# A transformer block with routed experts: another hand-written order for its beginning and its end, and the first sequence's q and k heads scaled on GpSimd

## The chip, the core and the metric

The kernel runs on one core of a Trainium2 chip. Its time is the device time of one execution in microseconds (us). TensorE (PE in the profile) multiplies matrices, VectorE (DVE) and ScalarE (ACT) read PSUM and SBUF, GpSimd (POOL) works on SBUF here, and SyncE (SP) issues DMA. Every engine takes its own instructions in the order in which the program gives them, and semaphores between engines make one wait for another.

## What is computed

Sixteen sequences of 256 tokens of width 256 pass through one attention block with 16 heads of 64. Then all 4096 tokens pass a routing step in which each of 8 experts picks its 512 best tokens:

```python
shift = jax.nn.silu(t) @ W_ada.T + b_ada
h = _ln(x, ln1_g, ln1_b) + shift
qkv = (h @ Wqkv.T).reshape(b, n, 3, H, HD)
q = _ln(q part, qn_g, qn_b); k = _ln(k part, kn_g, kn_b); v = v part
attn = softmax(q k^T / sqrt(HD)); x = x + (attn v) @ Wout.T
gate = softmax(tok @ Wgate.T, axis=-1)
vals, idx = top_k(gate.T, k_cap)
g = _ln(tok[idx_flat], mlp_g, mlp_b)
y = gelu(g @ fc1 + b1) @ fc2 + b2
tok = tok.at[idx_flat].add(y * w)
```

## The kernel before

All products are float32. The weights of q and k are first centred per head (`center`, L552 and L553, VectorE), so that the head's mean is already gone from the projection and only its variance is missing.

For each sequence, `First` normalises the two tiles of 128 tokens, transposes them (L597) and evicts them as `hT` (L605, ScalarE). A `Group` is one projection of 128 tokens to 512 columns, that is 8 heads: groups 0 and 1 are q, 2 and 3 are k, 4 and 5 are v. A v group is a matmul (L631) and a copy (L640). A q or k group has up to eight steps: `matmul` (L631), `square` (L644, ScalarE), `stats` (L648 and L652, VectorE), `power` (the power of -1/2, L82, GpSimd), `scale` (L664), `transposes` (L673), `evict` to `qT` or `kT` (L685, ScalarE), and, if an eighth place is given, `keep`: a copy of the projection from PSUM to SBUF (L626, ScalarE). `scale` looks whether `keep` has run. If it has not, VectorE multiplies straight out of PSUM, and if it has, GpSimd multiplies the copy:

```python
engine, src = nc.gpsimd, self.qk
if src is None:
    self.qk = work.tile([P, GW], F32, tag="qk", bufs=3, name="qk")
    engine, src = nc.vector, self.pm
```

A `Quad` is four heads in two pairs: scores (L706), row maxima (L713, VectorE), exponentials with their sums (L722, ScalarE), the inverse of the sums (L729), the normalising (L733, GpSimd), the transposes of the probabilities (L742), their copy out of PSUM (L750 on VectorE, L752 on ScalarE), the product with v (L760) and an eviction (L772, L770). A `Tail` projects 128 tokens back (L784), adds the residual (L791), writes the token to `out`, normalises it for the experts (L573) into `xn_dram`, and computes its gate logits (L806, L812, L817, L823).

PSUM has eight banks in this kernel: three buffers with the tag "mm" for projections and small transposes, four with the tag "sc" for scores, transposed probabilities and the experts, one with the tag "po".

The routing runs twice. Before the last sequence, the `first` search finds for each expert the 256th largest gate among the first 15 sequences: 30 steps of compare (L901, VectorE), count (L956, a small matmul), and `either` and `decide` (L962 and L971, VectorE), each waiting for the one before. `masks`, `scans`, `totals`, `place`, `turn_places` and `split` (L981 to L1025) then give each chosen token its place, one-hot columns (L1083 on VectorE, L1080 and L1081 on ScalarE) and small matmuls (L1091) turn the places into a list of token numbers, and a `Job` gathers the rows of `xn_dram` (L1107, GpSimd's queue), multiplies (L1116, L1135, L1142, L1151) and adds the result to `out` (L1168). There are 16 jobs: 8 experts on the first list, 8 on the second. The search and the first list stand beside the attention of the last sequence, and the second routing beside the first jobs, in an order that the code fixes.

The order of everything up to the first job is a plan written out by hand. Each step has a place, a number, and the steps are recorded in the order of their places. `STEADY` gives the places of one sequence, repeated with a period of 55.238. `START` replaces those of the sequences 0 to 3, `END` those of 12 to 15, and further tables (`SHIFT`, `CENTER`, `LOADS`, `EARLY`, `GATES`, `TURN`, `LOAD`, `SEARCH`, `PLACE`, `LIST`, `UP`, `DOWN`) place the rest. `FILL` sets how many transposes of a constant are put in at four points of the beginning.

## Time and profile before

| what | us |
|---|---|
| median of 3 runs (lowest to highest) | 1189.59 (1186.35 to 1192.12) |
| the profiled execution, device time | 1187.28 |
| its span, first to last instruction | 1185.6 |
| TensorE busy | 1157.4 |
| VectorE busy | 759.0 |
| ScalarE busy | 630.4 |
| GpSimd busy | 585.4 |

The profile is of one execution. Busy times are sums over instructions. The ends of matmuls are modelled, so the distance between the starts of two matmuls says more than their length. A waiting engine is put down to what released it last. In a row of busy times by stretch, the clock is what TensorE was granted as a share of full speed, followed by the share of DMA time and GB/s.

The mean granted clock is 0.994. The first matmul starts at 1.44 us, the search's first count stands at 864.89 us and its last at 906.96 us, the first expert's first matmul at 930.49 us.

### The profile page before, as it was taken

Reading aid. Unit: us, or ns where it says so; the run is one execution under the profiler, and the core shown is the slowest. Engines: PE = TensorE matmul, PEld = TensorE weight load, DVE = VectorE, ACT = ScalarE, POOL = GpSimd, SP = SyncE. Lnnn points to the kernel's source line nnn. Section 1 sums busy time; section 2 is a strip of 40 time slices with the busy share of each in tenths; the row PEclk is TensorE's granted clock in tenths of the full one; section 3 lists DMA queues with packets and bytes.
Section 4 is the critical chain, followed back from the end, with each engine's and each line's share of the span. In section 5 each row is a group of like instructions: output and inputs, shape, how many; then the busy total and the mean of one; then the engine's idle time right before and its main releaser. Section 6 shows DMA issues by size and latency. Waiting matters only on the chain. (4 is left out here: it accounts for less than half of the span.)

```text
span 1185.6 us, 19672 instructions
## 1 busy us (share of the span) xinstructions
PE 1157.4 (98%) x6823; PEld 817.5 (69%) x6823; DVE 759.0 (64%) x2303; ACT 630.4 (53%) x1721; POOL 585.4 (49%) x813
## 2 busy tenths in 40 slices
PE   8999999999999999999999999999988899999996
PEld 5566666666666666666666666677745788888885
DVE  7665676667566666666666666565588578755540
ACT  3856655566565656565655565656566333233331
POOL 3665464556556455555555545463672143333332
PEclk9999999999999999999999999999999999999998
DMA  6000000000000000000000000000110365666661
GB/s 197 1 1 6 5 19 19 10 19 10 19 23 6 23 10 19 10 23 6 23 10 27 10 10 9 19 14 19 61 39 1 113 190 183 187 187 187 183 187 21
DMA packets 46740, 62.41 MB, mean 53 GB/s; under 512 B 3889, under 2 KB 39985, under 8 KB 46641
## 3 DMA queue, kind: packets, MB, share of 16 engines
q1 hardware_dynamic: 36864, 49.03, 12.4%
q0 software_dynamic: 6144, 8.39, 3.9%
q10 hardware_dynamic: 3632, 3.74, 1.0%
q8 instruction: 54, 0.88, 0.3%
q14 instruction: 46, 0.37, 0.1%
HBM read 48.56 MB, written 12.58 MB: 52 GB/s over the span
## 5 line engine op out<-in xcount | busy, mean ns | idle before, releaser
L631 PE MATMUL pm<-wq,hT 128*128 128x512 f32 x768 | 361.8, 600 | 2.2 <-ACT qT L685 0.9
L733 POOL TENSOR_SCALAR pr<-pr,sums 128x256 f32<-128x256 f32 x512 | 236.9, 480 | 208.3 <-DVE sums L729 160.9
L82 POOL TENSOR_TENSOR ss<-ss,neghalf 128x8 f32<-128x8 f32 x128 | 211.8, 1656 | 184.7 <-DVE ss L652 180.0
L722 ACT ACTIVATE pr<-sc,nmax 128x256 f32<-128x256 f32 x512 | 236.2, 474 | 115.9 <-DVE nmax L713 108.3
L631 PEld LDWEIGHTS pm<-wq,hT 128*128 128x128 f32 x768 | 133.6, 190 | 123.4 <-issue 109.9
L713 DVE TENSOR_REDUCE nmax<-sc 128x2 f32<-128x512 f32 x256 | 166.7, 684 | 38.2 <-PE sc L706 38.1
L648 DVE TENSOR_REDUCE ss<-sq 128x8 f32<-128x512 f32 x128 | 87.4, 683 | 109.9 <-ACT sq L644 109.4
L742 PEld LDWEIGHTS pp<-ident,pr 128*128 128x128 f32 x1024 | 119.1, 142 | 48.2 <-POOL pr L733 21.0
L742 PE MATMUL pp<-ident,pr 128*128 128x128 f32 x1024 | 139.2, 274 | 0.1
L644 ACT ACTIVATE sq<-pm 128x512 f32<-128x512 f32 x128 | 76.7, 600 | 113.5 <-PE pm L631 110.1
L706 PE MATMUL sc<-kT,qT 64*128 64x256 f32 x1024 | 129.3, 390 | 0.0
L760 PE MATMUL po<-prT,v 128*64 128x256 f32 x1024 | 126.1, 389 | 0.0
L706 PEld LDWEIGHTS sc<-kT,qT 64*128 64x128 f32 x1024 | 93.3, 186 | 41.9 <-issue 31.1
L784 PE MATMUL pw<-wo,oT 128*128 128x256 f32 x512 | 117.8, 383 | 0.0
L1135 PE MATMUL ph<-xT,w 128*128 128x256 f32 x512 | 117.5, 382 | 0.0
L1151 PE MATMUL py<-w,hid 128*128 128x256 f32 x512 | 116.5, 380 | 0.0
L1168 POOL DMA_INDIRECT out<-y,idx x32 | 51.4, 1605 | 124.8 <-DVE y L1162 57.7
L784 PEld LDWEIGHTS pw<-wo,oT 128*128 128x128 f32 x512 | 96.7, 192 | 18.7 <-issue 6.5
L722 ACT ACTIVATION_READ_ACCUMULATOR pr<-sc,nmax 128x1 f32 x512 | 105.0, 205 | 0.0
L1142 ACT ACTIVATE hid<-ph,vec 128x256 f32<-128x256 f32 x128 | 60.2, 473 | 83.3 <-PE ph L1135 75.8
L1135 PEld LDWEIGHTS ph<-xT,w 128*128 128x128 f32 x512 | 95.4, 190 | 12.9
L1151 PEld LDWEIGHTS py<-w,hid 128*128 128x128 f32 x512 | 95.5, 190 | 12.7
(136 smaller groups left out, 1294.1 us busy)
## 6 DMA issues: line engine op xcount, KB each, us to landing
w<-in_fc2T SPq DMA_DIRECT2D x16, 1024.0 KB
w<-in_fc1T SPq DMA_DIRECT2D x16, 1024.0 KB
out<-tok SPq DMA_DIRECT2D x32, 128.0 KB
xn_dram<-tn SPq DMA_DIRECT2D x32, 128.0 KB
xs<-in_x SPq DMA_DIRECT2D x12, 256.0 KB
b<-in_b2s SPq DMA_DIRECT2D x16, 128.0 KB
wq<-in_wqkvT SPq DMA_DIRECT2D x3, 512.0 KB
wq<-in_wqkvT ACTq DMA_DIRECT2D x3, 512.0 KB
```

What stands on the lines that cost most here:

```text
L82: nc.gpsimd.tensor_tensor(dst, src, neghalf[:, : src.shape[1]], ALU.pow)
L631: nc.tensor.matmul(self.pm, hTs[self.b][:, c, bass.ts(self.t, P)], wq[:, c, bass.ts(self.g, GW)], start=(c == 0), stop=(c == DC - 1),)
L648: nc.vector.tensor_reduce(self.ss[:, 0, :], self.sq.rearrange("p (h d) -> p h d", d=HD), AX.X, ALU.add,)
L706: nc.tensor.matmul(self.sc[i, j][:, t, :], qTs[self.b][rows, hp, bass.ts(t, P)], kTs[self.b][rows, hp, :], start=True, stop=True,)
L713: nc.vector.tensor_reduce(self.nmax[i, j], self.sc[i, j], AX.X, ALU.max, negate=True)
L722: nc.scalar.activation(self.pr[i, j][:, t, :], self.sc[i, j][:, t, :], AF.Exp, bias=self.nmax[i, j][:, t : t + 1], scale=1.0, accum_out=se ...
L733: nc.gpsimd.tensor_scalar(self.pr[i, j][:, t, :], self.pr[i, j][:, t, :], self.sums[i][:, 1, j, t : t + 1], 1.0, ALU.mult, ALU.mult,)
L742: nc.tensor.transpose(self.pp[i, j][:, c, bass.ts(t, P)], self.pr[i, j][:, t, bass.ts(c, P)], ident,)
L760: nc.tensor.matmul(self.po[j * HD : (j + 1) * HD, i, :], vs[self.b][:, c, bass.ts(4 * self.d + 2 * i + j, HD)], self.prT[i, j][:, c, :], s ...
L784: nc.tensor.matmul(self.pw, oTs[self.b][:, hp, bass.ts(self.t, P)], wo[:, hp, :], start=(hp == 0), stop=(hp == HP - 1),)
L1135: nc.tensor.matmul(self.ph[f], self.w1[:, c, bass.ts(f, P)], self.xT[:, c, :], start=(c == 0), stop=(c == DC - 1),)
L1151: nc.tensor.matmul(self.py[i], self.hid[:, f, bass.ts(i, P)], self.w2[:, f, :], start=(f == 0), stop=(f == FC - 1),)
```

## The change

Numbers in the tables change, and no statement of the code. The tables `START` and `END` and all the further tables named above but `FILL` get new values (`STEADY` keeps its own), so the same steps stand in another order on each engine. Sequence 0's q and k groups get an eighth place, which means that `keep` is called: its eight projections are copied out of PSUM by ScalarE and scaled by GpSimd, where VectorE scaled them in PSUM. Sequence 15 does this already. The number of matmuls, transposes and fills is the same.

```diff
     START = {
         0: dict(
-            first=((-139.487, -139.084, -130.002), (-134.729, -123.135, -95.026), (-71.635, -61.204)),
+            first=((-133.593, -101.058, -97.256), (-158.376, -131.500, -104.051), (-81.952, -81.887)),
             group={
-                (0, 0): (-59.500, -57.180, -53.990, -41.905, -41.892, -31.199, -19.864),
-                (0, 1): (-56.514, -46.937, -42.187, -36.541, -32.975, -14.723, -12.430),
+                (0, 0): (-80.466, -69.038, -57.316, -39.709, -38.352, -36.469, -35.382, -52.242),
+                (0, 1): (-60.059, -54.606, -54.600, -39.627, -32.905, -30.429, -30.229, -51.780),
...
-    CENTER = ((-64.072, -68.386), (-36.649, -27.859), (-57.938, -59.128), (-18.701, -14.089))
+    CENTER = ((-91.311, -88.593), (-42.094, -51.590), (-84.871, -62.797), (-31.921, -44.332))
     FILL = (16, 4, 8, 12)
-    LOADS = (-61.203, -19.863)
+    LOADS = (-81.886, -35.381)
...
         15: dict(
...
             group={
-                (0, 0): (825.134, 835.486, 837.594, 846.062, 859.856, 877.526, 889.953, 847.485),
+                (0, 0): (839.140, 843.782, 846.873, 846.892, 851.911, 861.206, 869.747, 844.619),
...
-    EARLY = {14: (894.209, 902.691,), 15: (1025.834, 1032.355,)}
+    EARLY = {14: (910.717, 915.638,), 15: (1023.715, 1024.870,)}
...
-    PLACE = (1019.174, 1020.931, 1020.932, 1022.153, 1023.809, 1025.004, 1047.220)
+    PLACE = (1021.098, 1022.519, 1022.468, 1022.566, 1022.818, 1022.832, 1028.390,)
     LIST = (
-        dict(gives=1025.018, onehot=(1025.083, 1025.087, 1026.657, 1025.278, 1026.694, 1025.819,),
-             matmul=(1026.115, 1026.244, 1026.688, 1026.735, 1027.886, 1029.466,),
-             then=(1031.034, 1032.801, 1036.028, 1040.565,)),
+        dict(gives=1023.577, onehot=(1023.251, 1022.838, 1023.479, 1023.758, 1022.884, 1024.282,),
+             matmul=(1023.940, 1023.984, 1024.390, 1024.426, 1024.476, 1024.739,),
+             then=(1024.875, 1024.926, 1025.818, 1025.854,)),
```

On TensorE the beginning keeps its order up to the first q projection. Then five projections stand ahead of the first q/k transposes, where four stood. In the search, steps that had one transposed probability tile beside them now have two or none. Behind the search, the first job's list and its row transposes stand closer together, with less of the last projection between them: 0.86 us of it by the spacing of such matmuls in the profile, and the rest ahead of the second list.

## The prediction

> **What bounds the kernel now.** I read the page's busy shares first, then the same shares by stretch, then TensorE's waits, then its instructions in order of time.

> ```profile
> span 1185.6 us, 19672 instructions
> ...
> PE 1157.4 (98%) x6823; PEld 817.5 (69%) x6823; DVE 759.0 (64%) x2303; ACT 630.4 (53%) x1721; POOL 585.4 (49%) x813
> ```

> TensorE is busy for 98% of the span, and the change neither adds nor removes a matmul, a fill or a transpose. So only TensorE's lost time can move. A busy share hides part of that, because ends are modelled; I therefore price TensorE by the distance between starts. In time order, six 128x512 matmuls (two passes each) start at 31.86 us and the next group at 37.10: about 0.86 us per matmul when nothing waits. Likewise 0.109 us per 128x128 transpose, 0.22 per scores or value matmul, 0.43 per 128x256 expert or projection matmul. Counts times these give 1112 us; 73 us of the span are lost. In the steady middle the loss is about 1 us in 20, and the order of sequences 4 to 11 does not change. What stands out is the beginning and the stretch of the first threshold search.

> ```profile
> 10.00:20.00 10.00, 8.46 (x26) 3.69 (x24) 9.40 (x20) 2.41 (x5) 4.49 (x3) 1.00 0.41 151
> 20.00:30.00 10.00, 8.35 (x38) 4.72 (x40) 8.23 (x18) 5.28 (x9) 3.48 (x3) 1.00 0.61 185
> 30.00:40.00 10.00, 9.62 (x45) 5.11 (x42) 9.15 (x19) 8.00 (x26) 6.82 (x8) 1.00 0.01 2
> ```

> Columns: length, then busy PE, weight load, DVE, ACT, POOL, then clock. VectorE is nearly full, ScalarE and GpSimd are not: VectorE ends the waits here.

> ```profile
> PE pc L956 <- DVE reach L901: 7.1, 16, 0.8
> PE pls L1091 <- ACT oh L1081: 3.3, 5, 1.5
> ...
> PE pq L673 <- DVE qk L664: 1.3, 2, 1.0
> ...
> PE pm L631 <- ACT qT L685: 0.9, 1, 0.9
> ...
> PE pm L631 <- DVE wq L553: 0.7, 1, 0.7
> PE pm L631 <- DVE qk L664: 0.7, 1, 0.7
> ```

> The last four lines are the beginning, three of them VectorE's centring and scaling. The first two are the search and the job list behind it.

> ```profile
> 898.50:902.00 3.50, 2.74 (x24) 1.69 (x21) 3.32 (x16) 2.42 (x11) 1.58 (x5) 1.00 0.00 0
> 902.00:905.40 3.40, 2.12 (x16) 1.46 (x15) 2.89 (x16) 2.47 (x7) 1.36 (x3) 1.00 0.00 0
> 905.40:908.90 3.50, 2.35 (x18) 1.49 (x18) 3.20 (x17) 2.25 (x4) 1.84 (x4) 1.00 0.02 5
> 908.90:912.30 3.40, 3.40 (x18) 1.73 (x15) 1.58 (x5) 0.33 (x1) 0.00 (x0) 0.50 0.00 0
> ...
> 919.00:922.50 3.50, 0.72 (x4) 0.38 (x4) 0.45 (x2) 3.29 (x11) 0.00 (x0) 1.00 0.00 0
> 922.50:925.90 3.40, 3.40 (x23) 2.86 (x24) 2.77 (x18) 0.00 (x0) 2.00 (x2) 0.51 0.11 27
> ```

> The clock is granted at half twice (0.50 and 0.51), each time for 3.4 us after thinly filled stretches, costing some 1.7 us each on top of the waits.

> **The beginning.** For sequence 0, eight scalings (8 x 0.68 = 5.4 us) leave VectorE. In exchange ScalarE copies the projection out of PSUM and GpSimd scales the copy. Both steps exist in sequence 15 of this trace:

> ```profile
> L626 ACT COPY qk<-pm x8: 580/584/620, 833.6 to 872.5; 128x512 f32<-128x512 f32 x8
> L664 POOL TENSOR_TENSOR qk<-qk,ss x8: 1042/1042/1228, 835.3 to 877.4; 128x512 f32<-128x512 f32 x8
> ```

> So ScalarE gets 8 x 0.58 = 4.7 us and GpSimd 8 x 1.05 = 8.4 us. What matters is the PSUM buffer: "mm" has three. Before, a projection held one until square, statistics, power (1.65 us on GpSimd) and scaling were over: TensorE idles until 17.83 for `qk`, and until 20.79 for the first q/k transposes. After, it is held only until square and copy. I walked the new orders by hand with these durations and 0.2 to 0.3 us per hop. The first q projection starts at 10.9 instead of 11.75, as its first half of wq is now centred first. Five projections then run without a gap to 19.5. The first transposes start at 19.9: GpSimd does two powers (15.4 to 18.7) before the first scaling (to 19.8). The second half of the q weights is centred late, at 22.9: 0.95 us lost. The transposes of sequence 1 start at 35.4 with 30.2 us of work ahead of them, 5.1 lost; in the trace 41.29 with 32.4 ahead, 8.9 lost.

> Then part is given back. In the work from 20 to 40 us of TensorE, ScalarE's queue holds 23.8 us against 19.0 before. Behind its copies stand the evictions of q and k, of sequence 1's `hT`, and the exponentials that free the four "sc" buffers. I find 1.1 us lost at `hT` and 1.1 at the scores of quad 1. The four DMA issues in ScalarE's queue (0.4 to 0.5 us each) are moved too, past the v copy and a square; that is in the walk. At 41.5 us of work the loss is 7.4; before, 9.2: 1.8 gained, with bounds of 4 (nothing given back) and -2 (each hop longer by 0.2).

> [...] The row above has its worst scaling 0.19 us over its best, beside a VectorE busy with other operations; no centring ran beside it. [...]

> **Sequences 1 to 3 and 12 to 14.** The work of each engine per 20 us of TensorE work stays within the bounds of the steady middle, except GpSimd at 780 to 800 (19.4 against 11.8; less after it: 7.5 against 16.8). The old order lost only about 1 us in 20 here, so there is nothing to win; I take zero, up to 3 us lost. The loads of `xs` on SP move with them; the last is issued at 741.5 and first read at 769.8, 28 us of cover.

> **The search.** One step (L956, decide, compare) with 0.44 us of TensorE work beside it takes 1.12 to 1.16 us: VectorE's chain 0.28 + 0.54 + 0.09 and the hops. With 0.88 beside it 1.17, with 1.72 1.83, with 1.76 about 2.0. The old order takes 42.07 us between the first and last counting matmul, with 26.2 us of work beside them. The new one has 26.1 us, spread otherwise: only 7 steps of 29 with 0.44 (15 before), more with 0.87, and three with none at all where a maximum (0.68) sits in the chain. My sum is 41.4: 0.7 gained, bounds 3 and -2. Places alone save little, as the chain is VectorE's.

> **From the last count to the second expert.** Before, the first expert's list completes 16.0 us after the last count, because ScalarE's ten one-hot columns (0.63 each) wait at 915.52 for a PSUM eviction that TensorE orders late. After, five of them stand ahead of that eviction and start as soon as the places are split. The place matmul now waits for the scans with nothing beside it (2.1 to 3.6 after the last count: 1.5 lost). Split to 5.6, five columns to 8.8, eviction 0.6, five more to 12.5: list complete at 12.6, with TensorE nearly idle from 9.3. Then the projection (3.4), list two (waits 0.5 for VectorE's last column), 0.9 of projection: 18.4. Meanwhile take (0.3), two gathers (issued at 13.2 and 14.8, 3.4 to landing) make the rows at 18.2, so no wait; the eviction costs 0.3 more. The same point (the second expert's down matmuls, 954.78, or 47.8 after the last count) comes at 41.8, with 0.9 less work in it: 5.1 gained. The second expert's weights are issued on SP after the last projection, at 18.5; 2.1 MB at the 290 to 370 GB/s of the stretch 930 to 938 are 7 us and some 2 to start, so 28, and they are needed at 33.9.

> The clock decides how much remains. [...] I take 3.4.

> Sum: 1.8 + 0.7 + 3.4 = 5.9 us. The profiled execution took 1187.28 us (its span 1185.6 and 1.7 around it), 2.3 under the median of the runs, 1189.59. So 1181.4 for such an execution, and 1183.7 for the median.

> **The rivals.** (1) All of it holds: no half clock behind the list (1.7 more) and nothing given back to ScalarE at the start (2 more): 1180.0. For it: waits are short. Against it: the clock rows, and 23.8 us of ScalarE in 20. (2) The end's gain is spent: a second halving (1.7), and gathers landing 1.7 late because little stands between list and first rows: 1183.7 + 3.4 = 1187.1. Before, six us of projection covered them. (3) Slower: ScalarE's in-order queue at the start. In the first 50 us it was idle for 22.9, waiting mostly for projections. If copies placed ahead of evictions wait in turn, idle does not shrink while work to 40 us grows from 33.5 to 37.6: that point comes at 22.9 + 37.6 = 60.5 instead of 51.0, 9.5 us late; less the end's 4.1, 1195.0. It decides once ScalarE gives up less than 5.4 of its idle 22.9. Against it: seven of its waits (11.3 us, for projections) shrink when TensorE no longer waits for VectorE.

> **How the numbers follow.** The sum above 0.50 (1179 to 1188 by the bounds); rival 1 0.22; rival 2 0.15; rival 3 0.13. A measurement of this kernel can tell some 0.5% from no change: faster by over that is under 1183.6. That holds for rival 1 and half of the first case: 0.47; slower 0.13 (rival 3); within it 0.40. The range, 1177 to 1190, leaves out rival 3 and some of the far end.

> **What would show it.** The first q projection near 10.9 us and no TensorE wait for `qk` before 19; sequence 1's first transposes near 35; ScalarE over 90% busy from 30 to 45. First to last count 41 to 42 us. The list's end 12 to 13 us after the last count, one stretch of half clock after it. I am wrong if TensorE waits in sequences 12 to 14, or if the scalings on GpSimd take clearly over 1.05 us.

## The result and the profile after

| | before | after |
|---|---|---|
| median of five runs each (lowest to highest), us | 1190.09 (1186.35 to 1192.12) | 1183.99 (1182.07 to 1186.23) |
| profiled execution, us | 1187.28 | 1182.07 |

The ratio is 0.9952, with a 95% interval of 0.9936 to 0.9969: 0.3 to 0.6% faster. The forecast was 1183.7 us.

Executions of one kernel differ by how long the clock is halved in them: of the 51 runs of before that stand beside the experiments below, the 21 of at most 1188.12 us had a mean granted clock of 0.994 or 0.995 and the other 30 (1188.19 to 1192.12 us) one of 0.990 to 0.993, so ratios are safer than single times.

The page's span and busy shares:

```profile
span 1180.3 us, 19683 instructions
...
PE 1155.7 (98%) x6823; PEld 816.9 (69%) x6823; DVE 755.3 (64%) x2295; ACT 632.7 (54%) x1729; POOL 593.2 (50%) x821
```

VectorE has eight instructions less, ScalarE and GpSimd eight more each, TensorE the same number; its busy time falls by 1.7 us, which is what one stretch of half clock less (3.4 us) would give. The gain is lost time of TensorE, counted as in the prediction (distance between starts less the spacing of such a matmul), by stretch:

| TensorE's lost time, us | before | after | difference | predicted |
|---|---|---|---|---|
| start to 60 us | 8.15 | 6.19 | -1.96 | -1.8 |
| 60 us to the first count | 38.20 | 38.42 | +0.22 | 0 |
| first count to last count | 15.24 | 13.59 | -1.65 | -0.7 |
| last count to the second expert's down matmuls | 10.62 | 8.96 | -1.66 | -3.4 |
| the rest | 3.17 | 3.16 | 0 | 0 |
| sum | 75.38 | 70.32 | -5.06 | -5.9 |

The beginning, busy time by stretch (length, then TensorE, weight load, VectorE, ScalarE, GpSimd, then the clock):

```profile
10.00:20.00 10.00, 10.00 (x35) 4.94 (x34) 9.66 (x20) 4.29 (x8) 4.61 (x4) 1.00 0.41 150
20.00:30.00 10.00, 8.80 (x32) 4.43 (x31) 7.61 (x19) 6.36 (x12) 9.46 (x9) 1.00 0.58 186
30.00:40.00 10.00, 10.00 (x49) 5.67 (x48) 6.60 (x16) 9.08 (x24) 9.04 (x9) 1.00 0.00 1
40.00:50.00 10.00, 10.00 (x53) 6.03 (x52) 6.51 (x14) 9.54 (x35) 7.26 (x13) 1.00 0.00 0
```

Read it against the three rows of before: TensorE has no gap from 10 to 20, where it had 1.54 us. From 20 on GpSimd is full and from 30 on ScalarE is, the two engines that took VectorE's scalings; TensorE is full beside them, so they are close to the bound but not over it.

TensorE's waits (us in total, times, longest):

```profile
PE pc L956 <- DVE reach L901: 6.7, 10, 1.0
PE pls L1091 <- ACT oh L1081: 1.7, 4, 0.5
PE px L1116 <- DMA xg<-xn_dram,idx: 1.6, 1, 1.6
...
PE pm L631 <- ACT v L640: 1.2, 1, 1.2
PE pplace L1013 <- DVE place L1004: 1.0, 1, 1.0
```

All waits for VectorE's scaling and centring are gone; the list's wait for ScalarE's columns is halved. New are the projection's wait at 23.2 us behind the copy of v and that of the place matmul behind the scans. The wait for the second expert's rows has grown from 0.8 to 1.6 us; the prediction's sum has no term for it, and it is most of what is missing at the end. In before it was:

```profile
PE px L1116 <- DMA xg<-xn_dram,idx: 0.8, 1, 0.8
```

The transfers and that wait in after, in order of time:

```profile
923.43 1.00 POOL L1107 DMA_INDIRECT xg<-xn_dram,idx  x1 [2.40 <-DVE w L1102]
...
924.15 0.38 SPq L1053 DMA_DIRECT2D w<-in_fc2T  x1
924.59 0.73 SPq L1055 DMA_DIRECT2D w<-in_fc1T  x1
924.74 0.95 POOL L1107 DMA_INDIRECT xg<-xn_dram,idx  x1 [0.30 <-issue]
...
931.86 0.33 PE L1116 MATMUL px<-ident,xg 128*128 128x128 f32 x1 [1.57 <-DMA xg<-xn_dram,idx]
```

The two gathers and the 2 MB of weights between them are all the second expert's. Its second gather is issued behind the weights and its rows come 7.1 us later. The weights themselves came in time.

One stretch of half clock is left behind the list. The rows are cut at the moments at which the clock changes, and at the same distance before them (the clock is the third figure from the end):

```profile
906.47:909.88 3.41, 2.39 (x22) 1.80 (x23) 2.31 (x6) 1.56 (x3) 0.35 (x1) 1.00 0.00 0
909.88:913.29 3.41, 3.41 (x22) 2.57 (x18) 3.37 (x21) 3.20 (x11) 0.54 (x2) 1.00 0.00 0
913.29:916.70 3.41, 1.74 (x31) 1.07 (x29) 3.11 (x19) 3.25 (x11) 0.00 (x0) 1.00 0.02 5
916.70:920.12 3.42, 3.21 (x9) 2.58 (x10) 2.86 (x15) 0.16 (x1) 2.21 (x2) 0.50 0.13 36
```

### The profile page after: what moved, and what is told of

The parts are those of the page before. It is cut to its first block, busy times and chain, and to the rows that moved or that the text cites. A ratio compares the mean times of both kernels' runs of the same rounds, so it can differ in the third digit from the quotient of the medians.

```text
span 1180.3 us, 19683 instructions
## 1 busy us (share of the span) xinstructions
PE 1155.7 (98%) x6823; PEld 816.9 (69%) x6823; DVE 755.3 (64%) x2295; ACT 632.7 (54%) x1729; POOL 593.2 (50%) x821
## 3 DMA queue, kind: packets, MB, share of 16 engines
q1 hardware_dynamic: 36864, 49.03, 12.5%
## 5 line engine op out<-in xcount | busy, mean ns | idle before, releaser
L631 PE MATMUL pm<-wq,hT 128*128 128x512 f32 x768 | 360.5, 599 | 1.2 <-ACT v L640 1.2
L631 PEld LDWEIGHTS pm<-wq,hT 128*128 128x128 f32 x768 | 133.4, 190 | 120.3 <-issue 108.0
L706 PEld LDWEIGHTS sc<-kT,qT 64*128 64x128 f32 x1024 | 93.7, 186 | 38.2 <-issue 26.1
L1135 PEld LDWEIGHTS ph<-xT,w 128*128 128x128 f32 x512 | 95.3, 190 | 13.2 <-ACT xT L1123 0.4
```

Of the source, the lines that this page charges most:

```text
L631: nc.tensor.matmul(self.pm, hTs[self.b][:, c, bass.ts(self.t, P)], wq[:, c, bass.ts(self.g, GW)], start=(c == 0), stop=(c == DC - 1),)
L706: nc.tensor.matmul(self.sc[i, j][:, t, :], qTs[self.b][rows, hp, bass.ts(t, P)], kTs[self.b][rows, hp, :], start=True, stop=True,)
L1135: nc.tensor.matmul(self.ph[f], self.w1[:, c, bass.ts(f, P)], self.xT[:, c, :], start=(c == 0), stop=(c == DC - 1),)
```

## The experiments

My theory after the result: three places gave the gain (the projections' PSUM buffers at the beginning, the search, the earlier list), each about as in the table, and at the end a part was spent on the half clock and on the collision of the gather with the weights. The rivals: the copies on GpSimd do nothing and the places everything; the new end alone carries the gain; the half clock or the wait for rows is only a symptom of the late list.

The runs of before beside them had medians of 1190.09 us (24 runs, beside the first four experiments), 1189.33 (16, beside the next four) and 1188.12 (11, beside the last three), in the order below. In what follows, "the point" is the start of the second expert's down matmuls, and a ratio is to the kernel before.

**Only the beginning.** The kernel before with `START`, `SHIFT`, `CENTER` and `LOADS` of the kernel after; `END` and all tables behind it are the old ones:

```diff
-            first=((-139.487, -139.084, -130.002), (-134.729, -123.135, -95.026), (-71.635, -61.204)),
+            first=((-133.593, -101.058, -97.256), (-158.376, -131.500, -104.051), (-81.952, -81.887)),
...
-    LOADS = (-61.203, -19.863)
+    LOADS = (-81.886, -35.381)
```

> The new places of the beginning, with sequence 0's heads scaled on GpSimd, and the old places of the end. Theory (the two ends of the change add up): 2.2 us of the 5.3 us of span are the beginning's, so the span is 1183.4. Rival (the beginning is only lent: what it wins is waited for later): 1185 to 1186.

Measured: 1186.80 us, ratio 0.9978 (0.9965 to 0.9990), span 1186.3. From last count to the second expert's down matmuls it lost 12.30 us, before 10.62, in the same order of instructions: the half clock came twice there too, but the second time for 6.8 us. Up to 60 us it lost 7.49, not 6.19, and that lies in the first 10 us, which are the same in both: matmuls had double spacing until 10 us in this execution and until 5.4 us in the profile of after.

**Only the end.** The reverse, with the new values in `END` and all tables behind it, and the old ones ahead of it:

```diff
-    EARLY = {14: (894.209, 902.691,), 15: (1025.834, 1032.355,)}
+    EARLY = {14: (910.717, 915.638,), 15: (1023.715, 1024.870,)}
...
-    LOAD = (908.722, 1034.995)
+    LOAD = (917.376, 1025.786)
```

> The old beginning and the new places of the end. Theory: 3.1 us of the span are the end's, 1182.5. Rival (the end's order only fits a beginning that is as early): 1184 or more.

Measured: 1187.69 us, ratio 0.9984 (0.9972 to 0.9997), span 1186.0. From first to last count 40.59 us (after 40.41, before 42.07), from last count to the point 45.28 (after 45.29): what the end gives, it gives alone. But up to 60 us this execution lost 10.90 us against 8.15 in the profile of before, with the same instructions in the same order. The rows by stretch show a part of why:

```profile
20.00:24.00 4.00, 2.15 (x8) 0.88 (x7) 3.93 (x8) 1.37 (x2) 2.84 (x3) 1.00 0.01 2
24.00:27.50 3.50, 3.50 (x7) 1.53 (x7) 3.36 (x9) 0.38 (x1) 0.60 (x1) 0.53 0.98 311
```

Behind a thin stretch (2.15 of 4.00 us) the clock was halved here for 3.4 us, and in the profile of before it was not. The other part is the start: matmuls had double spacing until 10.7 us here and until 4.4 us in the profile of before. Both spans missed what I expected, by 2.9 and 3.5 us, and the half clock and the double spacing account for most of it: they belong to the execution and not only to the kernel. The ratios multiply to 0.9962, beside 0.9952 for both together: within the intervals the two parts add. Each interval ends below 1, so neither part is nothing; how much each gives is not told finer than that.

**The kernel after without the copies.** The eighth place of sequence 0 is taken out, so its eight scalings are VectorE's in PSUM again, at the new places:

```diff
-                (0, 0): (-80.466, -69.038, -57.316, -39.709, -38.352, -36.469, -35.382, -52.242),
+                (0, 0): (-80.466, -69.038, -57.316, -39.709, -38.352, -36.469, -35.382),
...
```

> The changed kernel with sequence 0's q and k heads scaled on VectorE out of PSUM at the same places. Theory (the copy frees the PSUM buffer early, and that is what the beginning wins): the five projections no longer run through, TensorE waits for qk again, and the span is 1183 to 1185, 2 us or more over the changed kernel's 1180.3. Rival (the new places alone win it, the copy is incidental): 1180 to 1181.

Measured: 1203.15 us, ratio 1.0113 (1.0092 to 1.0133). TensorE's waits:

```profile
PE pm L631 <- DVE qk L664: 6.0, 1, 6.0
PE pq L673 <- DVE qk L664: 4.0, 3, 3.3
PE pm L631 <- ACT kT L685: 2.7, 3, 0.9
```

The direction is the theory's, the size is not: 19 us worse than after, where I had expected to lose little more than the gain. The places are made for a PSUM buffer that is free early; with the buffer held, the fourth of the five projections stands still for 6.0 us and all behind it with it. Up to 60 us TensorE loses 25.79 us. Not all of that is waiting: the clock was halved from 21.14 to 27.97 us and from 45.03 to 48.44, in and behind the long waits, and the first matmuls had double spacing until 11.0 us.

**The kernel before with the copies.** The other corner: the copy right behind the square, the scaling on GpSimd, every other place old:

```diff
-                (0, 0): (-59.500, -57.180, -53.990, -41.905, -41.892, -31.199, -19.864),
+                (0, 0): (-59.500, -57.180, -53.990, -41.905, -41.892, -31.199, -19.864, -57.178),
...
```

> The kernel before with one thing added: sequence 0's projections are copied right behind the square and scaled on GpSimd, at the old places. Theory (GpSimd's scaling is slower, 1.05 against 0.68 us, and behind powers of 1.65, so without new places it comes late): the first transposes wait longer, 1186 to 1189. Rival (VectorE's relief alone wins it): 1183.4.

Measured: 1193.72 us, ratio 1.0041 (1.0024 to 1.0057), slower than before. The wait came as expected, but it was longer: the span is 1191.1, above the 1186 to 1189 of the theory. The wait:

```profile
PE pq L673 <- POOL qk L664: 6.6, 2, 6.2
```

A scaling on GpSimd comes later than on VectorE (copy, then 1.04 us instead of 0.68, behind the powers), and the old order has q's transposes right behind: TensorE stands 6.2 us at one of them, and the clock is halved for 6.8 us right behind it (from 24.72 us). So neither the copies nor the places give anything alone. The copies free the PSUM buffer early and give the scaled heads late; the new order uses the first (five projections in a row) and hides the second behind the same projections.

**The weights behind the gather.** The second expert's weights are issued on SP one output tile later:

```diff
-    LOAD = (917.376, 1025.786)
+    LOAD = (917.376, 1025.8125)
```

> The changed kernel with the second expert's weights issued behind the second token write of sequence 15 in SP's queue, some 2 us later. Theory (the 1.57 us wait for the second expert's rows is a collision: 2 MB of weights are issued at 924.15, ahead of the gathers of 923.43 and 924.74, and fill the DMA engines): the rows land some 3.4 us after their issue, the wait is under 0.5, and the span is 1.2 to 1.6 us shorter, if the clock's halvings are the same. Rival (the gather is late because its indices are late): the wait stays at 1.6.

Measured: 1180.78 us, ratio 0.9925 (0.9905 to 0.9946). The gather now goes out ahead of the weights, its rows land 4.5 us after the issue (more than the 3.4 expected, less than the 7.1 of after), and the same transposes have no wait:

```profile
925.86 0.96 POOL L1107 DMA_INDIRECT xg<-xn_dram,idx  x1 [0.30 <-issue]
926.14 0.39 SPq L1053 DMA_DIRECT2D w<-in_fc2T  x1
...
931.11 0.63 PE L1116 MATMUL px<-ident,xg 128*128 128x128 f32 x4
```

The last count to the point takes 44.80 us, although half clock lasted 6.8 us here and 3.4 in after. The wait was a collision, and its remedy is the order of two issues. The times alone don't show it: the interval overlaps that of after.

**The late columns on VectorE.** The first job's last five one-hot columns go from ScalarE, where they stood behind the PSUM eviction, to VectorE; another group of five, VectorE's already, is moved forward there:

```diff
-                engine = nc.scalar if a is jobs[0] and k in (2, 5) else nc.vector
+                engine = nc.scalar if a is jobs[0] and k == 2 else nc.vector
...
-        dict(gives=1023.577, onehot=(1023.251, 1022.838, 1023.479, 1023.758, 1022.884, 1024.282,),
+        dict(gives=1023.577, onehot=(1023.251, 1022.838, 1023.479, 1023.500, 1022.884, 1023.550,),
```

> The changed kernel with the last five one-hot columns of the first list on VectorE, ahead of the second list's, so that ScalarE makes only five. Theory (the list is ScalarE's: 10 columns of 0.63 around an eviction): the list completes at 914.4 instead of 917.0, TensorE has no stretch of 3 us with little work and the clock is not halved there. Of the 4 us that this is worth at most, 1 to 2 reach the span, since take still stands behind the second list's columns on VectorE. Rival (the list's end is set by the places): still 917.

Measured: 1181.87 us, ratio 0.9940 (0.9920 to 0.9960); span 1178.5. TensorE around the two lists:

```profile
913.95 0.90 PE L1091 MATMUL pls<-give,oh 128*128 128x10 bf16 x30 [0.18 <-DVE oh L1083]
914.70 3.70 PE L784 MATMUL pw<-wo,oT 128*128 128x256 f32 x16
...
920.56 0.84 PE L1091 MATMUL pls<-give,oh 128*128 128x10 bf16 x5 [0.81 <-DVE oh L1083]
```

The list is complete at 914.7 us, as expected; of the five gaps that TensorE had in after's first list one is left (0.18 us). VectorE is late with the second list instead (0.81 us), and the half clock moves there. The point comes 43.18 us after the last count, 2.1 earlier than in after. The second gather went out at 923.19, ahead of the weights (923.70), and its rows came without a wait.

**The columns behind the eviction.** The five columns that the change moved ahead of that eviction go back:

```diff
-        dict(gives=1023.577, onehot=(1023.251, 1022.838, 1023.479, 1023.758, 1022.884, 1024.282,),
+        dict(gives=1023.577, onehot=(1023.251, 1022.838, 1023.930, 1023.758, 1022.884, 1024.282,),
```

> The changed kernel with all ten columns of ScalarE behind the last eviction of the attention, as in the kernel before. Theory: the columns start at about 911.4 instead of 909.94, so the list ends 1.0 to 1.5 us later (918 to 918.5), and the span is about that much longer. Rival (the order of eviction and columns is not what moved the list; the earlier product is): within 0.3 us.

Measured: 1185.02 us, ratio 0.9966 (0.9953 to 0.9978); the list ends 1.0 us later against the last count (13.5 us, 12.5 in after), and the point is 47.49 us after it, against 45.29. The last matmul of the list here, with the last count at 904.84:

```profile
918.29 0.19 PE L1091 MATMUL pls<-give,oh 128*128 128x10 bf16 x1 [0.44 <-ACT oh L1081]
```

The 2.2 us are the later list and a half clock that lasts 6.8 us here instead of 3.4; one profile can't part the two. So the place of these five columns ahead of the eviction is worth 1.0 us of the list; what of that reaches the point is not parted from the clock.

**Filling the gap.** Sixteen transposes of the identity, which nothing reads, stand ahead of the first list's matmuls, where TensorE would wait:

```diff
+        at([1023.935], partial(fill, 16))
         for a, p in zip(jobs, LIST[:2]):
```

> The changed kernel with 16 transposes of a constant (1.7 us) on TensorE ahead of the first list's matmuls, where it waits anyway. They add work that nothing reads. Theory (the half clock follows a stretch that is thinly filled, and costs 1.4 to 1.7 us): no halving behind the list, the span 1.4 to 1.7 shorter than with one. [...]

Measured: 1182.57 us, ratio 0.9941 (0.9921 to 0.9960). The clock around the list:

```profile
914.00:917.50 3.50, 3.50 (x45) 3.28 (x44) 3.46 (x22) 3.38 (x11) 0.00 (x0) 1.00 0.02 5
917.50:921.00 3.50, 2.84 (x26) 2.41 (x23) 2.81 (x18) 1.02 (x4) 1.37 (x2) 1.00 0.00 0
921.00:924.50 3.50, 3.50 (x47) 3.10 (x46) 2.49 (x13) 0.00 (x0) 2.36 (x3) 1.00 0.39 112
```

No half clock is left: with work that computes nothing the end was 1.1 us shorter (44.20 to the point), although TensorE waited 0.5 us more for the rows. The times do not tell this run from after, but the profiles do: all eleven without fills at the lists have half clock behind one of the two, and the two with fills, this one and the last of these runs, have none. So the half clock there follows from the thin list, with its own price.

**The wait at 23 us.** Two places in the beginning:

```diff
-    CENTER = ((-91.311, -88.593), (-42.094, -51.590), (-84.871, -62.797), (-31.921, -44.332))
+    CENTER = ((-91.311, -88.593), (-51.590, -42.094), (-84.871, -62.797), (-31.921, -44.332))
...
-    LOADS = (-81.886, -35.381)
+    LOADS = (-81.886, -32.200)
```

> The kernel after with two places changed in the beginning: wq's first half of head group 1 is centred before its second half, and the last four loads that ScalarE issues go behind the copy of v. Theory (the wait of 1.20 us at 23.2 us is a tie of two: the copy of v, queued behind four DMA issues, and the half of wq that is centred last but needed first): the wait shrinks to 0.6 to 0.8, the copy of v begins at 22.1 instead of 22.5, and the stretch 20 to 40 us loses about 0.5 us less; the median falls by 0.3 to 0.6, which the times can hardly show. Rival (only the centring counted, and the copy came in its shadow): the wait shrinks by less than 0.1. A late arrival of the third sequence's tokens, whose load is now issued later, would show as a wait of VectorE's statistics behind a DMA.

Measured: 1182.55 us, ratio 0.9949 (0.9934 to 0.9964); as foreseen, the times can't tell it from after. In its trace the wait is gone altogether, but matmuls had double spacing until 9.5 us, so TensorE came later to this place while VectorE did not. The cleaner comparison is that of the next two kernels, one with the old places and one with these.

**Both edits at the end.** The weights behind the gather and the late columns on VectorE, each diff as above.

> The kernel after with both edits that were run alone: the second expert's weights issued behind the gather's indices, and the first job's last two groups of columns on VectorE. Each alone gave 1180.8 and 1181.9 beside 1184.0. Theory (they act at two places and add): the list is complete at 914.7, the first product of the gathered rows of job 1 has no wait, and the down products of the second expert begin 40.0 to 40.5 us behind the matmul that follows the last count; median 1178.5 to 1180.5. Rival (both take the same time back, through one clock halving and one wait): no better than 1180.5.

Measured: 1179.97 us, ratio 0.9926 (0.9911 to 0.9941). The median is in the theory's range, below the rival's 1180.5, but the runs of before beside it were lower too: the ratio is no better than with the weights alone (0.9925), and the point is 43.13 us after the last count, as with the columns alone (43.18). The expectation had counted from the first matmul of `totals` (L996, at 907.10 us): 41.16 here instead of 40.0 to 40.5. The two do not add: with the list earlier, the gather went out ahead of the weights anyway. The rival's cause fits, its number does not.

**Everything.** The beginning of the run above, both edits at the end, and eight such fills ahead of the second list:

```diff
+        at([1025.345], partial(fill, 8))
         for a, p in zip(jobs, LIST[:2]):
```

> All of it: the beginning of the run above, both edits at the end, and eight transposes of the identity, which nothing reads, ahead of the second list's matmuls, where TensorE waits for columns anyway. Theory: the two waits in the second list (0.16 and 0.81 us in the run with the columns on VectorE) are filled, the halving behind them is gone, and 1.7 us go with it when it would have come; median 1177.5 to 1179.5, which would be the fastest here. Rival (the fills come on top, 0.9 us, and the halving follows other idle time): 1179 to 1181, with a halved window between 917 and 926.

Measured: 1178.34 us (1177.31 to 1179.42), ratio 0.9915 (0.9900 to 0.9929), whose interval ends where that of after (0.9936 to 0.9969) has not begun: faster than both kernels. TensorE in the beginning, first with both edits at the end, then with everything:

```profile
23.89 1.53 PE L631 MATMUL pm<-wq,hT 128*128 128x512 f32 x3 [1.20 <-ACT v L640]
```

```profile
23.74 1.12 PE L631 MATMUL pm<-wq,hT 128*128 128x512 f32 x2 [0.30 <-DVE wq L553]
```

With the first half centred first and the copy of v ahead of the DMA issues, 0.90 of the 1.20 us are gone. The run changes both at once; that one alone would not have done it is read from the times of after's trace, where the two end together (below). At the end the clock stays full, and the point comes 41.81 us after the last count, 1.3 earlier than with both edits and 3.5 earlier than in after. Which part of the gain in the median is whose, no run tells.

## Why the prediction was right, and where not

The sum was 5.9 us and 5.06 came; the forecast for the median was 0.3 us off. That it came so close is luck in part: of its terms two were clearly off and partly cancelled, since the search gave 0.95 more than said and the end 1.74 less.

- **The beginning: right.** First q projection 11.02 us (10.9 said), five projections without a gap to 19.65 (19.5), sequence 1's first transposes at 35.68 (35.4), ScalarE 9.08 and 9.54 of 10 busy from 30 to 50; 1.96 us gained for 1.8. The mechanism, the PSUM buffer freed by the copy, holds with its counterpart that I had not put so sharply: the two corner runs show it only in the order made for it. The 1.96 itself is of one pair of executions, and its closeness to 1.8 is luck in part: up to 60 us the old order lost 10.90 us in another execution (8.15 in this one), the new order 7.49 (6.19).
- **Rival 3, ScalarE's queue, did not come, and its sum was wrong.** For the kernel before, its 22.9 us of idle and 33.5 of work would give 56.4 us, where it has 51.0 itself. Busy times leave DMA issues out, and ScalarE makes eleven in that time (5.3 us by the trace); they seem to stand in both figures, so the 60.5 is some 5 us too late.
- **The loss on wq's centring: the size right (1.20 for 0.95), the cause half.** I had the four DMA issues in the walk, and still named the centring alone. They held the copy of v, and with it a PSUM buffer, until the same moment: the copy ends at 23.12 us, the centring at 23.09, the matmul starts at 23.19.

```profile
21.38 1.11 ACTq L490 DMA_DIRECT2D xs<-in_x  x2
...
22.27 0.82 DVE L553 SCALAR_TENSOR_TENSOR wq<-ws,wq 128x512 f32<-128x512 f32 x1
22.54 0.58 ACT L640 COPY v<-pm 128x512 f32<-128x512 f32 x1 [0.42 <-issue]
```

  What was to be given back at `hT` and at the scores came mostly as this wait: from 20 to 40 us TensorE lost 2.56 us, from 40 to 60 us 1.36.
- **VectorE beside GpSimd's scalings: longer instructions showed, no wait put down to them.** Two scalings in a row, from 21.27 us on, took 1.27 and 1.49 us where the median is 1.04, and the centring above, beside the end of the one and the start of the other, 0.82 for 0.69:

```profile
L664 POOL TENSOR_TENSOR qk<-qk,ss x16: 1038/1042/1486, 18.5 to 873.6; 128x512 f32<-128x512 f32 x16
```

  A small statistics instruction of VectorE, beside a scaling that ran from 18.52 to 19.56, took five times its usual 0.17 and ended with the scaling:

```profile
18.68 0.90 DVE L652 TENSOR_SCALAR ss<-ss 128x8 f32<-128x8 f32 x1
```

  No TensorE wait of the list above is put down to these delays (0.1 to 0.7 us each). Three centrings were left when the scalings began, and two of them, at 20.95 and 22.27 us, met a scaling, each for a part of it; the first kept its 0.69. I had looked at the row of sequence 15 alone, and it showed too little, since nothing of this kind ran beside it. What made these instructions longer is not shown.
- **The search: 1.65 for 0.7.** First to last count took 40.41 us, not 41.4. I had priced three steps without any matmul beside them longer, for a maximum in VectorE's chain; they took 1.12 to 1.13, like the shortest. Ten waits for VectorE of up to 1.0 us stand where sixteen of up to 0.8 stood. The gain comes with the end's places alone (40.59 in that run), so that "places alone save little" was too low; but no run took the search's places apart.
- **The list: right.** Complete 12.5 us after the last count (12.6), one half-clock stretch instead of two; putting the five columns back made it 13.5.
- **The failed step: the wait for the second expert's rows, a term that the sum leaves out.** My "so no wait", with gathers at 13.2 and 14.8 and 3.4 us to landing, is about the first expert's rows, and they came without a wait (the gathers went out 13.2 and 14.7 us after the last count). For the second expert I followed the weights alone. Its gathers went out 19.0 and 20.3 us after the last count, the weights between them at 19.7, and the rows cost 1.57 us; the run with the weights behind takes that away. Before had already lost 0.8 us at this wait. Rival 2 gave a late gather 1.7, close to what came, but meant the first expert's rows: the size was luck. With 1.57 off, the end's 3.4 becomes 1.8, and 1.66 was measured.
- **The half clock: right.** The end's 3.4 was my estimate: the 5.1 of the earlier list less 1.7 for one stretch of half clock, since in before's rows TensorE was busy for 2.35 of 3.50 and 0.72 of 3.50 us ahead of the two halvings. One stretch came, behind a list whose longest wait was 0.45 us, and filling the gap took it away. The 1.7 us for one stretch fits the profile; not every execution has it at the same place or length.

Left open: what decides on the clock between a full and a thin stretch. Cut as above, the stretch ahead of after's half clock had TensorE busy for 1.74 of 3.41 us. But in the run with both edits 2.58 us (919.59 to 923.00) was followed by half clock, and in before 2.05 (878.16 to 881.57) was not. So the busy time of one stretch doesn't decide alone.

## What to carry to other kernels

The copies freed a buffer earlier and handed on its result later, and alone they made the kernel slower (ratio 1.0041), as did the new order alone (1.0113): change both together, and when you test such a step, test both corners. When a change brings a small urgent transfer forward, look at which big one now stands ahead of it in time, even on another queue (here 2 MB of weights, and a wait of 1.57 us). Thin stretches of TensorE cost twice here, once as waits and once as clock, and filling the one ahead of the first list made the end 1.1 us shorter, so an idle gap that can't be closed may be worth filling.
